# Attention on one Trainium2 core: the negated row maxima reach the queries by two DMAs instead of transposes on TensorE

## The chip, the cores and the metric

The kernel runs on one NeuronCore of a Trainium2 chip. Its engines are named as in the profile: PE (TensorE, the matrix products; PEld is its weight load), DVE (VectorE), ACT (ScalarE), POOL (GpSimd) and SP (SyncE, which here only issues DMAs). The metric is the device time of one execution, in microseconds (us), as the median of several runs.

## The reference

The input is `x` of shape (8, 192, 64, 64): 8 images, 192 channels, 4096 pixels. Two layers follow each other, each added to its input.

```
def _L0_conv_ref(x, w1, b1, a1, w2, b2, a2, wa, ba, aa):      # 1x1 convolutions to 24, 24 and 192 channels
    q = prelu(conv1x1(x, w1, b1), a1)
    k = prelu(conv1x1(x, w2, b2), a2)
    v = prelu(conv1x1(x, wa, ba), aa)
    q = q.reshape(b, -1, hw).transpose(0, 2, 1)
    k = k.reshape(b, -1, hw)
    score = jax.nn.softmax(jnp.einsum('bnc,bcm->bnm', q, k), axis=2)
    v = v.reshape(b, c, hw).transpose(0, 2, 1)
    out = jnp.einsum('bnm,bmc->bnc', score, v)
...
x = x + _L0_conv_ref(_gn(x), ...)     # _gn: normalization over groups of 6 channels
x = x + _L1_conv_ref(_gn(x), ...)     # pointwise: four small linear maps with tanh between them, then
                                      # abs(sigmoid(sign * upper) - sigmoid(sign * lower)), at least 1e-6
```

So layer 0 is attention over 4096 pixels per image, with 24 channels of queries and keys and 192 of values, all in float32. Layer 1 is elementwise work with per-channel weights (below: the density).

## The kernel before

**Blocks and steps.** Each image has 8 blocks of 512 queries, so there are 64 blocks. A block takes 16 steps; a step handles 256 keys for the block's 512 queries. `scores` (L794) computes two products of 128 keys by 512 queries into PSUM, ACT takes their exponential (L798), and `attend` (L809) multiplies the exponentials with the values: 8 products of 128 queries by 193 columns, the last column being the sum of the row. The main loop runs the 1024 steps one after the other; the head before it prepares image 0, and the tail after it finishes the density of image 7.

**The maxima.** The softmax subtracts each query's maximum before the exponential. The maxima of a block are found ahead: in every step, `max_step` (L722, L730) computes 128 queries by 1024 keys, for the step that lies `LEAD` = 22 steps further, and DVE reduces them. After 16 such steps a block's maxima are complete, 6 steps before its first scores. The queries lie in a tile `q` with 128 partitions: four groups of 32, each with 24 channels and one row more, row 24 of the group (`CR`). The keys have a 1 in that row, so a score product over 25 rows adds whatever stands there. The negated maximum of each query has to get there.

**How it gets there now.** `max_end` (L744) plans three things. `collect`: DVE reduces 16 columns to 4 and negates (L750), and copies the result into columns 24, 56, 88, 120 of a tile `negmax` that is zero otherwise (L753). `turn`: PE transposes `negmax` in four 128x128 pieces into a PSUM bank (L759). `add`: DVE adds this bank to the block's columns of `q` (L765), where only the four rows 24 get anything but zero. `turn` needs a free half of a PSUM turn tile, so it goes through `job`, a queue of pieces of work (keys L634, values L683, transposed outputs L842) of which `start_job` starts one a step.

**What sets the order.** The order on every engine is written by the program itself. `at(t, fn, cost, act, pe)` puts a function into step `t`; `work_off` runs the step's functions, starts one job, issues the loads for which a buffer is free, and lets the density take what is left: `density_step` gives DVE and ACT as much density work as a credit allows, which falls with the planned cost of the other work and rises with the time planned for PE. Nothing else reorders. SP issues its DMAs strictly in this order: loads of `x` for statistics, keys and values (`xi`, L109) and for the residual (`xc`, L109, four DMAs of 384 KB at once), stores of finished keys and queries (L649, L650), loads of the queries of two blocks (`queries`, L665), and stores of the output (L1374). A tile's reader waits for the DMA that wrote it.

**Other places that the change touches.** `weights` folds the normalization into the convolutions, once per image: `mb` (L554) is the mean of each channel copied along 128 columns, and `products` multiplies it with the weights of the values (L566). The partitions hold the 64 rows of channels twice; `products` uses the first 64. Before the first products, the head waits for the statistics of image 0.

Of the kernel before, what the change touches and what calls it, by code (L numbers as in the profile page):

```python
# [9 lines left out]
F32 = mybir.dt.float32  # L10
AF = mybir.ActivationFunctionType
ALU = mybir.AluOpType
# [5 lines left out]
def kernel(  # L18
# [43 lines left out]
    nc = tc.nc  # L62

    B, C, H, W = x.shape
    N = H * W
    CR = w1t.shape[1]
    F = 512
# [4 lines left out]
    R = C // 3  # L72
# [9 lines left out]
    const = ctx.enter_context(tc.tile_pool(name="const", bufs=1))  # L82
# [7 lines left out]
    dram = ctx.enter_context(  # L90
        tc.tile_pool(name="dram", bufs=1, space=bass.MemoryType.DRAM)
    )
    dens = ctx.enter_context(tc.tile_pool(name="dens", bufs=1))
    ps_sc = ctx.enter_context(tc.tile_pool(name="ps_sc", bufs=1, space=PSUM))
    ps_mx = ctx.enter_context(tc.tile_pool(name="ps_mx", bufs=1, space=PSUM))
# [3 lines left out]
    for i in range(2):  # L99
        turn = ps_b.tile([128, 2, F], F32, tag=f"b{i}", name=f"b{i}")  # L100
# [17 lines left out]
    for i in range(3):  # L118
        t = xin.tile([128, 3, P], F32, tag=f"xi{i}", name=f"xi{i}")
# [20 lines left out]
    ident = const.tile([128, 128], F32, name="ident")  # L140
    make_identity(nc, ident)


    gavg = const.tile([128, 128], F32, name="gavg")
    gq = gavg.rearrange("p (s a b) -> p s a b", s=2, b=2)
    idq = ident.rearrange("p (s a b) -> p s a b", s=2, b=2)
# [31 lines left out]
    for i in range(2):  # L178
        nc.vector.tensor_reduce(
            out=bb[i], in_=ident[:, 64 * i + CR : 64 * i + 64 : 32], axis=AX.X, op=ALU.add  # L180
# [6 lines left out]
    for s in range(2):  # L187
        p = slice(R * s, R * s + R)
# [4 lines left out]
    for i in range(2):  # L193
# [3 lines left out]
        for k in range(2):  # L197
            a = a2 if k == i else a1
            nc.scalar.dma_start(
                out=slope[i][64 * k : 64 * k + 64], in_=a.partition_broadcast(64)  # L200
# [3 lines left out]
    def spread():  # L204

        for i in range(2):
            for k in range(4):
                at = slice(32 * k, 32 * k + CR)
                p = slice(R * (k % 2), R * (k % 2) + R)
                nc.gpsimd.tensor_copy(wr[i][p, :, at], (s2 if k // 2 == i else s1)[p])  # L210
        for g in range(3):
            nc.gpsimd.tensor_copy(
                wa_sb[:, g, :].rearrange("p (h r) -> p h r", h=3),
                sa[:, g, :].rearrange("p (r h) -> p h r", h=3),
            )
        for s in range(2):
            p = slice(R * s, R * s + 1)
            nc.gpsimd.tensor_copy(
                ba_row[p].rearrange("p (h r) -> p h r", h=3),
                sb[p].rearrange("p (r h) -> p h r", h=3),  # L220
            )

    def negatives():
        for i, a in enumerate((*slope, vslope)):
            nc.vector.tensor_scalar(nslope[:, i : i + 1], a, -1.0, None, ALU.mult)

    negmax = const.tile([128, 4, 128], F32, name="negmax")
    nc.gpsimd.memset(negmax, 0.0)


    mm = const.tile([128, 3, 24], F32, name="mm")
# [2 lines left out]
    for src, dst, at, n in (  # L234
# [4 lines left out]
        for s in range(2):  # L239
            nc.sync.dma_start(  # L240
                out=dst[R * s : R * s + R, :, at : at + n],
                in_=src.rearrange("(r g) i j -> r g (i j)", g=3),
# [84 lines left out]
    now = [0]  # L327

    def at(t, fn, cost=0.0, act=0.0, pe=0.0):

        due.setdefault(max(t, now[0]), []).append((fn, cost, act, pe))
# [13 lines left out]
    def job(make, hold, rank=3, banks=1, cols=0):  # L345

        jobs.append((rank, make, hold, banks, cols))
        jobs.sort(key=lambda j: j[0])  # L350
# [9 lines left out]
    for k in "ab":  # L360
        pair = []
        for i in range(2):
            u = work.tile([128, 2 * C], F32, tag=f"pr{k}{i}", name=f"pr{k}{i}")
# [7 lines left out]
    def spotted():  # L371

        n, i = spot[0]

        def write(inst):
            tc.declare_no_dep(inst.ins, group=f"turn{n}{1 - i}", reason="reads the other bank")

        def read(inst):
            tc.add_to_no_dep_group(f"turn{n}{i}", inst.ins)

        return write, read
# [159 lines left out]
    wf = {}  # L541

    def weights(b, then):
        res = norms[b, 0]
        cell = {}

        def scale():
            for k, src in ((0, wr[0]), (1, wr[1]), ("v", wa_sb)):
                d = wf[k, b] = fold.tile(
                    [128, 3, src.shape[2]], F32, tag=f"w{k}", name=f"w{k}_{b}"  # L550
                )
                nc.scalar.activation(d, src, AF.Copy, scale=res[:, 1:2])
            mb = cell["mb"] = fold.tile([128, 128], F32, tag="mb", name=f"mb_{b}")
            nc.vector.tensor_copy(mb, res[:, 0:1].to_broadcast([128, 128]))  # L554

        def products():
            pf = cell["pf"]
            p = slice(0, R)
            for i in range(2):
                for g in range(3):  # L560
                    cell["write"](nc.tensor.matmul(
                        pf[:, 2 * i : 2 * i + 2], lhsT=wf[i, b][:, g, :], rhs=res[:, 0:2],
                        start=g == 0, stop=g == 2,
                    ))
            for g in range(3):
                cell["write"](nc.tensor.matmul(  # L566
                    pf[:, 4 : 4 + C], lhsT=cell["mb"][p], rhs=wf["v", b][p, g, :],
                    start=g == 0, stop=g == 2,
                ))

        def offsets():
            pf = cell["pf"]
            for i in range(2):
                d = wf["b", i, b] = fold.tile([128, 2], F32, tag=f"b{i}", name=f"b{i}_{b}")
                cell["read"](nc.vector.tensor_tensor(
                    d[:, 0:1], bb[i], pf[:, 2 * i : 2 * i + 1], ALU.subtract
                ))
                nc.vector.tensor_scalar(d[:, 1:2], d[:, 0:1], -1.0, None, ALU.mult)
            d = wf["ba", b] = fold.tile([128, C], F32, tag="ba", name=f"ba_{b}")
            cell["read"](nc.vector.tensor_tensor(d, ba_row, pf[:, 4 : 4 + C], ALU.subtract))  # L580
            then()

        at(now[0] + 1, scale, 0.3, 2.0)

        def make(pf, _):
            cell["pf"] = pf
            cell["write"], cell["read"] = spotted()
            return [(0, products, 0.0, 0.0, 2.0), (1, offsets, 1.0, 0.0, 0.0)]

        at(now[0] + 3, lambda: job(make, 1))  # L590
# [5 lines left out]
    for i in range(NC + 2):  # L596
        v = vpool.tile([128, 2, 4, C + 1], F32, tag=f"v{i}", name=f"v{i}")
        nc.gpsimd.memset(v[:, :, :, C : C + 1], 1.0)
        vtiles.append(v)
    qt = {}  # L600
# [18 lines left out]
    for i in range(2):  # L619
        t = dram.tile([NC, 64, F], F32, tag=f"qd{i}", name=f"qd{i}")  # L620
# [113 lines left out]
    def max_step(m):  # L734
        b, n, j, k = place(m)
        if b >= B:
            return
        sc = ps_mx.tile([128, 2, F], F32, tag="mx", name=f"mx_{m}")
        max_products(b, n, j, k, sc)
        max_reduce(b, n, j, k, sc)  # L740
        if m % STEPS == STEPS - 1:
            max_end(b, n)

    def max_end(b, n):  # L744
        rm = small.tile([128, 4], F32, tag="rn", name=f"rn_{b}_{n}")
        nm = negmax
        cell = {}

        def collect():
            nc.vector.tensor_reduce(  # L750
                out=rm, in_=rowmax.pop((b, n)), axis=AX.X, op=ALU.max, negate=True
            )
            nc.vector.tensor_copy(nm[:, :, CR::32], rm.unsqueeze(2).to_broadcast([128, 4, 4]))  # L753

        def turn():
            pt = cell["pt"]
            for t in range(4):
                cell["write"](
                    nc.tensor.transpose(pt[:, t * 128 : (t + 1) * 128], nm[:, t, :], ident)  # L759
                )  # L760

        def add():
            u = (n % 2) * 256
            q = qt[b, n // 2][:, :, u : u + 256]
            cell["read"](nc.vector.tensor_tensor(  # L765
                q, q, cell["pt"].rearrange("p (s t) -> p s t", s=2), ALU.add
            ))
            made.add(("max", b, n))

        def make(pt, _):  # L770
            cell["pt"] = pt
            cell["write"], cell["read"] = spotted()
            return [(0, turn, 0.0, 0.0, 0.8), (1, add, 0.7, 0.0, 0.0)]

        at(now[0], collect, 0.4)
        at(now[0] + 1, lambda: job(make, 1, 0))


    ex = {}
# [711 lines left out]
    while todo or ahead:  # L1491
        if todo:
            make, d, *k = todo.pop(0)
            make(0, d, *k, "first", lambda: None)
        pair = list(zip(others, ahead.popleft() if ahead else ()))
        if pair and len(homes) > 2:
            del homes[2:]
        for t, (n, j, k) in pair:
            max_products(0, n, j, k, t)
        for t, (n, j, k) in pair:  # L1500
            max_reduce(0, n, j, k, t)
        if (0, 3, 3) in [i for _, i in pair]:
            max_end(0, 0)
        if ("qd", 0, 1) in made and (0, 0) not in qt:
            queries(0, 0)
        go_on()
# [9 lines left out]
    for t in range(last):  # L1516
        b = t // IMG
# [21 lines left out]
    t = last  # L1539
# [42 lines left out]
```

## Time and profile before

| what | value |
|---|---|
| runs | 4770.4, 4772.68 and 4775.0 us; median 4772.68 us |
| the profiled execution | 4769.2 us, of which the span of instructions is 4767.4 us |
| first score product starts | 89.9 us |
| main loop to the start of the last score product | 4419.2 us |
| PE busy | 4627.5 us, 97% of the span |
| DVE busy | 4166.2 us, 87% |
| ACT busy | 3220.1 us, 68% |
| transposes of the maxima (L759) | 256 products, 38.4 us of busy time |
| their addition to the queries (L765) | 64 instructions, 43.4 us of DVE |
| DMA queue of SP | 133.81 MB, 11.5% of the 16 engines' time |

A row of the profile's groups reads: line, engine, operation, output and inputs by name, shapes and how often; then the busy time, the mean duration of one in nanoseconds, and the engine's idle time in front of it with what ended it. A float32 product appears as two MATMUL rows (and two LDWEIGHTS), a transpose as one. The timeline gives start, duration and count; equal instructions that follow each other are merged into one row.

### The profile page before, as it was taken

How to read it: one execution, taken by the hardware profiler on the slowest of the kernel's cores; microseconds unless marked ns; L12 is line 12 of the kernel's file. 1: busy time of each engine (PE TensorE's matmuls, PEld its weight loads, DVE VectorE, ACT ScalarE, POOL GpSimd, SP SyncE). 2: the span in 40 equal slices, each digit the busy share in tenths (PEclk: the TensorE clock that was granted, in tenths of full speed). 3: DMA queues.
4: the chain of work that ended last, by engine and by line, in shares of the span. 5: the costliest groups of instructions: out<-in, count | busy, mean ns of one | idle time of the engine just before them, and what ended most of it. 6: DMA issues, size and time to landing. Idle time of an engine off the chain costs nothing.

```text
span 4767.4 us, 68896 instructions
## 1 busy us (share of the span) xinstructions
PE 4627.5 (97%) x28344; PEld 3428.8 (72%) x28344; DVE 4166.2 (87%) x4289; ACT 3220.1 (68%) x3687; POOL 865.6 (18%) x842
## 2 busy tenths in 40 slices
PE   7999999999999999999999999999999999999685
PEld 5777777777777777777777777777777777777332
DVE  5433359999999999999999999999999999998898
ACT  2332246767677777776777767777777777778786
POOL 0000001212222212221212222132222122232100
PEclk9999999999999999999999999999999999999797
DMA  2101020111100111110110111001111101000000
GB/s 59 41 18 30 18 48 14 33 30 30 44 25 25 37 39 34 27 40 12 36 46 26 30 41 36 28 16 40 36 38 33 31 16 27 10 5 23 9 14 13
DMA packets 109328, 138.58 MB, mean 29 GB/s; under 512 B 17107, under 2 KB 82133, under 8 KB 109013
## 3 DMA queue, kind: packets, MB, share of 16 engines
q1 hardware_dynamic: 107776, 133.81, 11.5%
q8 instruction: 222, 3.64, 0.3%
q14 instruction: 94, 0.76, 0.1%
q10 hardware_dynamic: 1236, 0.37, 0.0%
HBM read 100.58 MB, written 29.36 MB: 27 GB/s over the span
## 4 chain that ended last, share of the span: by engine, by line
PE 93%; DVE 3%; ACT 2%; issue 1%; DMA 0%; POOL 0%; ACTq 0%; POOLq 0%; SPq 0%; DVEq 0%
PE b L809 60%; PE sc L794 22%; PE b L683 4%; DVE d L1094 2%; PE b L634 2%; PE mx L722 1%; PE b L1033 1%; PE b L842 1%; PE mx_tail L1033 1%; PE b L759 1%; ACT d L1087 0%; PE sc_tail L1033 0%; ACT d L1062 0%; ACT e L798 0%; ACT d L1077 0%
## 5 line engine op out<-in xcount | busy, mean ns | idle before, releaser
L809 PEld LDWEIGHTS b<-v,e 128*128 128x128 f32 x16384 | 2650.6, 190 | 776.4 <-issue 765.1
L809 PE MATMUL b<-v,e 128*128 128x193 f32 x16384 | 2954.5, 334 | 0.0
L798 ACT ACTIVATE e<-sc 128x1024 f32<-128x1024 f32 x1024 | 1045.4, 1021 | 1320.2 <-PE mx L722 1282.7
L730 DVE TENSOR_REDUCE rm<-mx 128x1 f32<-128x1024 f32 x1002 | 1223.4, 1221 | 476.6 <-PE mx L722 470.3
L794 PE MATMUL sc<-q,k 25*128 25x512 f32 x4096 | 1154.6, 640 | 4.1 <-ACT e L798 3.8
L722 PE MATMUL mx<-k,q 24*128 24x512 f32 x4008 | 1129.8, 640 | 0.0
L1094 DVE SCALAR_TENSOR_TENSOR d<-d,lc,d 128x1024 f32<-128x1024 f32 x756 | 977.3, 1302 | 16.8 <-ACT d L1071 4.8
L1094 DVE SCALAR_TENSOR_TENSOR d<-d,wsp,d 128x1024 f32<-128x1024 f32 x684 | 877.4, 1286 | 44.9 <-ACT d L1087 36.5
L1277 POOL MEMSET pause<- 128x1 f32 x408 | 39.9, 98 | 3585.2 <-DVE d L1094 3585.2
L1094 DVE SCALAR_TENSOR_TENSOR d<-d,tf,d 128x1024 f32<-128x1024 f32 x540 | 685.4, 1288 | 2.3 <-ACT d L1077 2.3
L1077 ACT ACTIVATE d<-d 128x1024 f32<-128x1024 f32 x540 | 566.8, 1052 | 40.1 <-DVE d L1094 39.6
L794 PEld LDWEIGHTS sc<-q,k 25*128 25x128 f32 x4096 | 306.2, 182 | 229.6 <-issue 188.9
L1087 ACT ACTIVATE d<-d,cb,wsp 128x1024 f32<-128x1024 f32 x348 | 429.3, 1235 | 1.6 <-DVE d L1094 0.6
L1062 ACT ACTIVATE d<-xc,bn,wn 128x1024 f32<-128x1024 f32 x288 | 354.3, 1234 | 0.8 <-issue 0.8
L1125 POOL TENSOR_TENSOR d<-d,d 128x512 f32<-128x512 f32 x168 | 335.9, 2000 | 37.1 <-ACT d L1119 35.7
L1071 ACT ACTIVATE d<-xc,bn,wn 128x1024 f32<-128x1024 f32 x252 | 311.4, 1236 | 0.0
L722 PEld LDWEIGHTS mx<-k,q 24*128 24x128 f32 x4008 | 299.6, 182 | 9.1 <-DVE rm L730 8.2
L1312 POOL TENSOR_TENSOR d<-d,d 128x512 f32<-128x512 f32 x80 | 170.1, 2127 | 0.0
L1324 POOL TENSOR_TENSOR d<-d,d 128x512 f32<-128x512 f32 x80 | 169.9, 2124 | 0.5 <-issue 0.5
L1332 POOL TENSOR_TENSOR d<-d,d 128x512 f32<-128x512 f32 x80 | 159.2, 1990 | 1.8
L683 PE MATMUL b<-wv,xi 64*128 64x192 f32 x1344 | 139.5, 340 | 0.0
L683 PEld LDWEIGHTS b<-wv,xi 64*128 64x128 f32 x1344 | 106.5, 186 | 25.4 <-issue 23.6
(158 smaller groups left out, 2288.6 us busy)
## 6 DMA issues: line engine op xcount, KB each, us to landing
xi<-in_x_dram SPq DMA_DIRECT2D x280, 192.0 KB, 3.7
xc<-in_x_dram SPq DMA_DIRECT2D x64, 384.0 KB, 7.5
out_dram<-xc SPq DMA_DIRECT2D x94, 256.0 KB, 3.2
q<-qd SPq DMA_DIRECT2D x128, 128.0 KB, 2.7
k<-kq SPq DMA_DIRECT2D x64, 64.0 KB, 1.9
qd<-kq SPq DMA_DIRECT2D x64, 64.0 KB, 2.1
d<-in_x_dram SPq DMA_DIRECT2D x16, 192.0 KB, 4.2
out_dram<-xc SPq DMA_DIRECT2D x4, 128.0 KB
```

The lines of the kernel that those rows point to most:

```text
L683: nc.tensor.matmul(pv[:, s, 0:C], lhsT=t[p, g, k * 128 : k * 128 + 128] if g < 3 else one_row[p], rhs=wf["v", b][p, g, :] if g < 3 else wf ...
L722: nc.tensor.matmul(sc[:, s, :], lhsT=tile_of(qt[b, n // 2], n, j)[r], rhs=kt[b][r, u : u + F], start=True, stop=True,)
L730: nc.vector.tensor_reduce(out=rowmax[b, n][:, j, k : k + 1], in_=sc, axis=AX.XY, op=ALU.max)
L794: nc.tensor.matmul(sc[:, s, :], lhsT=kt[b][r, k : k + 128], rhs=qt[b, n // 2][r, :, u : u + 256], start=True, stop=True,)
L798: return lambda: nc.scalar.activation(e, sc, AF.Exp)
L809: nc.tensor.matmul(a[:, j, 0 : C + 1], lhsT=e[:, s, j * 128 : j * 128 + 128], rhs=v[:, s, p % 4, :], start=p == 0 and s == 0 and j % 2 == ...
L1062: nc.scalar.activation(self.buf[k], self.src(), AF.Tanh, bias=bn[:, s, g, 0, i : i + 1], scale=wn[:, g, 0, i : i + 1],)
L1071: nc.scalar.activation(self.buf[k], self.src(), AF.Identity, bias=bn[:, s, g, 1, i : i + 1], scale=wn[:, g, 1, i : i + 1],)
L1077: nc.scalar.activation(self.buf[k], self.buf["l", k[1], k[2]], AF.Tanh)
L1087: nc.scalar.activation(self.buf[k], self.buf["l", n - 1, 0], AF.Identity, bias=offset, scale=wsp[:, g, w : w + 1],)
L1094: nc.vector.scalar_tensor_tensor(dst, src, factor, dst, ALU.mult, ALU.add)
L1125: return nc.gpsimd.tensor_tensor(z[:, n], z[:, n], dst[:, n], ALU.add)
```

## The change

`max_end` no longer uses PE. `collect` keeps only the reduction. Two steps later SP stores the 128x4 result to a DRAM tile of 4x128 (`nd`, two in turn), and four steps after `collect` SP loads it into row 24 of each of the four groups of `q`, one DMA for each. The transposes, the addition, the copy and `negmax` are gone, and with them one job a block. In the head, 14 products of the identity with itself, 384 columns each, are put in front of everything on PE; nothing reads them. `mb` is now half of the mean, and `products` sums over all 128 partitions instead of 64, which gives the same.

```diff
+    idle = ps_mx.tile([128, 2, F], F32, tag="mx", name="idle")
+    for i in range(14):
+        nc.tensor.matmul(
+            idle[:, i % 2, 0:384], lhsT=ident, rhs=ident.unsqueeze(1).to_broadcast([128, 3, 128]),
+            start=True, stop=True,
+        )
...
-    negmax = const.tile([128, 4, 128], F32, name="negmax")
-    nc.gpsimd.memset(negmax, 0.0)
...
-            nc.vector.tensor_copy(mb, res[:, 0:1].to_broadcast([128, 128]))
+            nc.vector.tensor_scalar(
+                mb, res[:, 0:1].to_broadcast([128, 128]), 0.5, None, ALU.mult
+            )
...
-                    pf[:, 4 : 4 + C], lhsT=cell["mb"][p], rhs=wf["v", b][p, g, :],
+                    pf[:, 4 : 4 + C], lhsT=cell["mb"], rhs=wf["v", b][:, g, :],
...
+    nd = []
+    for i in range(2):
+        t = dram.tile([4, 128], F32, tag=f"nd{i}", name=f"nd{i}")
+        nd.append(t)
+
     def max_end(b, n):
...
-            nc.vector.tensor_copy(nm[:, :, CR::32], rm.unsqueeze(2).to_broadcast([128, 4, 4]))
-
-        def turn():
-            pt = cell["pt"]
-            for t in range(4):
-                cell["write"](
-                    nc.tensor.transpose(pt[:, t * 128 : (t + 1) * 128], nm[:, t, :], ident)
-                )
-
-        def add():
-            u = (n % 2) * 256
-            q = qt[b, n // 2][:, :, u : u + 256]
-            cell["read"](nc.vector.tensor_tensor(
-                q, q, cell["pt"].rearrange("p (s t) -> p s t", s=2), ALU.add
-            ))
+        d = nd[n % 2]
+
+        def store():
+            nc.sync.dma_start(out=d.rearrange("j p -> p j"), in_=rm)
+
+        def spread():
+            u = (n % 2) * 256
+            for k in range(4):
+                nc.sync.dma_start(
+                    out=qt[b, n // 2][32 * k + CR : 32 * k + CR + 1, :, u : u + 256],
+                    in_=d.rearrange("(o s) p -> o s p", o=1).rearrange(
+                        "o (s a) p -> o s (a p)", s=2
+                    ),
+                )
             made.add(("max", b, n))
 
-        def make(pt, _):
-            cell["pt"] = pt
-            cell["write"], cell["read"] = spotted()
-            return [(0, turn, 0.0, 0.0, 0.8), (1, add, 0.7, 0.0, 0.0)]
-
-        at(now[0], collect, 0.4)
-        at(now[0] + 1, lambda: job(make, 1, 0))
+        at(now[0], collect, 0.3)
+        at(now[0] + 2, store)
+        at(now[0] + 4, spread)
```

More of the change, by code (lines that the diff above doesn't have):

```diff
@@ L553, in scale @@
             mb = cell["mb"] = fold.tile([128, 128], F32, tag="mb", name=f"mb_{b}")
-            nc.vector.tensor_copy(mb, res[:, 0:1].to_broadcast([128, 128]))
+            nc.vector.tensor_scalar(
+                mb, res[:, 0:1].to_broadcast([128, 128]), 0.5, None, ALU.mult
+            )
         def products():
             pf = cell["pf"]
-            p = slice(0, R)
             for i in range(2):
@@ L742, in max_step @@
             max_end(b, n)
+    nd = []
+    for i in range(2):
+        t = dram.tile([4, 128], F32, tag=f"nd{i}", name=f"nd{i}")
+        nd.append(t)
     def max_end(b, n):
         rm = small.tile([128, 4], F32, tag="rn", name=f"rn_{b}_{n}")
-        nm = negmax
-        cell = {}
         def collect():
```

## The prediction

> **What bounds the kernel now.** First the busy times and the chain that ended last (page, parts 1 and 4):
>
> ```profile
> PE 4627.5 (97%) x28344; PEld 3428.8 (72%) x28344; DVE 4166.2 (87%) x4289; ACT 3220.1 (68%) x3687; POOL 865.6 (18%) x842
> PE 93%; DVE 3%; ACT 2%; issue 1%; DMA 0%; POOL 0%; ACTq 0%; POOLq 0%; SPq 0%; DVEq 0%
> ```
>
> The chain runs on PE for 93%, and no DMA is on it. Busy shares alone don't tell what a removed product is worth, so the timeline of PE is read around one `turn`:
>
> ```profile
> 410.19 0.70 PE L794 MATMUL sc<-q,k 25*128 25x512 f32 x2
> ...
> 413.98 0.60 PE L759 MATMUL b<-ident,negmax 128*128 128x128 f32 x4
> 414.51 0.70 PE L794 MATMUL sc<-q,k 25*128 25x512 f32 x2
> ...
> 415.58 2.88 PE L809 MATMUL b<-v,e 128*128 128x193 f32 x16
> 418.39 0.70 PE L794 MATMUL sc<-q,k 25*128 25x512 f32 x2
> ```
>
> A step from scores to scores takes 418.39 - 414.51 = 3.88 us, the one with the transposes 414.51 - 410.19 = 4.32. In this stretch PE waits for nobody, so a `turn` costs its 0.44 us in full.
>
> Then what goes or comes, from the groups:
>
> ```profile
> L765 DVE TENSOR_TENSOR q<-q,b 128x512 f32<-128x512 f32 x64 | 43.4, 679 | 0.0
> L753 DVE COPY negmax<-rn 128x16 f32<-128x16 f32 x64 | 16.2, 253 | 2.2
> L759 PE MATMUL b<-ident,negmax 128*128 128x128 f32 x256 | 38.4, 273 | 1.1 <-DVE negmax L753 1.1
> ```
>
> The 38.4 us are not the saving; the 64 steps are.
>
> Last the queue that the new DMAs enter, at block 6 of image 3: SP's timeline, then the landings there, in a window around 1584 (block 6 of image 2), and overall:
>
> ```profile
> 2121.66 1.12 SPq L1374 DMA_DIRECT2D out_dram<-xc  x2
> 2125.49 3.10 SPq L109 DMA_DIRECT2D xc<-in_x_dram  x4
> 2130.86 1.72 SPq L665 DMA_DIRECT2D q<-qd  x4
> ```
> ```profile
> xc<-in_x_dram SPq DMA_DIRECT2D x4, 384.0 KB, 7.9
> ```
> ```profile
> q<-qd SPq DMA_DIRECT2D x4, 128.0 KB, 6.6
> ```
> ```profile
> q<-qd SPq DMA_DIRECT2D x128, 128.0 KB, 2.7
> ```
>
> Seen over the span DMA is 11.5% busy, but here the engines are full for over 10 us: the same load of queries lands after 6.6 us behind the `xc` loads and after 2.7 us in the median. A DMA on SP's queue waits for the bytes in front of it.
>
> **The sum, part by part** (against the profiled execution, 4769.2 us, of which the span is 4767.4; the median of the runs is 4772.7, 3.5 higher).
>
> *Transposes.* 64 x 0.436 = -27.9 us, since the step is longer by that and PE is the bound (0.436 = 4.32 - 3.88 before rounding). The bounds are -38.4 (their busy time) and 0.
>
> *DVE.* 43.4 + 16.2 = 59.6 us of work go. Nearly all lay beside PE's products: DVE is 87% busy, PE 97%. It counts where DVE ends last. Near the start of block 1 of image 3, between 1781.8 and 1794.6, the three steps last 4.1, 4.2 and 4.5 us with DVE busy for 3.93, 4.20 and 4.50 of them: some 1.2 us over 3 x 3.88. Images 2 to 6 look alike there, so 5 x 1.2 = 6 us bounds the gain, 0 is the other end; the add stands just ahead of these steps, so I take half, -3.
>
> *Five DMAs a block.* One store of 128x4 elements of 4 bytes, four loads of two runs of 1 KB. Issuing costs SP about 0.6 (as the head's small loads: 8 in 5.15 us) + 4 x 0.43 = 2.3 us, on an engine that mostly waits. `collect` ends about 22 us before the block's first scores, e.g. `rn` at 2112.7 and scores at 2134.23. The store is put in two steps later, the load four, so that the load may go when SP has passed all that was planned up to two steps before the scores, and the store has landed. The store has no like in the trace. A 64 KB store of queries lands after 2.1 us; the head's loads of 64 single elements after 3.1. With 3 to 4 us for the store and 2.3 for a load, most blocks keep 6 to 20 us. Even at 8 x (3.1 - 2.1) = 8 us for 512 single elements on top only two or three us appear in a dozen blocks; so this is kept for the range, up to +20.
>
> What is exposed are the blocks where SP's queue has the refill of `xc` between store and load: two output stores, which wait for DVE (2121.66), and four loads that wait for these stores (2125.49). In the changed order this holds for blocks 2 and 6 of images 2 to 6. At block 6 of image 3 the new loads are issued from 2128.6 to 2130.3, behind 1.57 MB. The fourth `xc` load, issued about 2128.0, lands 7.9 us later, at 2135.9; the bytes alone (at the 205 to 230 GB/s that the window shows, from 2126.2) are through by 2133.4, and an engine of the 16 that finishes early lets a small load through at about 2134.5. The scores stood at 2134.23 and come 0.44 earlier for the `turn` that was between: 2133.8. So they wait 0.7 to 2.3, I take 1.5. Block 6 of images 2, 4, 5, 6 has the same spacing (first `xc` load 8.7 to 8.8 us before the scores): 5 x 1.5 = 7.5. Block 2 of images 3 to 6 has 10.3 to 12.3 us there, so 0 to 0.8 each; image 7 has a store behind an `xc` refill, 0 to 1.2: together 1.5. Block 2 of image 2 loses more: its refill is planned one step later than before, 3.9 us, so its first `xc` load comes some 8 us before the scores, or 6.5 when the half-clock stretch below is gone: 4. Sum +13; bounds 0 (small loads slip through) and +30 (ten times 3).
>
> *Clock.* The granted clock fell to half twice in the loop, after stretches of small products (L561, then L566 on 64 of 128 rows):
>
> ```profile
> 1295.50:1298.90 3.40, 3.40 (x28) 2.71 (x27) 3.37 (x4) 0.00 (x0) 0.00 (x0) 1.00 0.48 110
> 1298.90:1302.30 3.40, 3.40 (x13) 2.86 (x10) 2.88 (x8) 2.71 (x3) 0.00 (x0) 0.50 0.27 91
> 90.60:94.00 3.40, 1.15 (x10) 0.31 (x8) 0.62 (x1) 2.56 (x3) 0.00 (x0) 1.00 0.00 0
> 94.00:97.40 3.40, 3.40 (x13) 2.85 (x10) 1.23 (x1) 1.02 (x1) 0.00 (x0) 0.50 0.00 0
> ```
>
> (busy us and count of each engine, then granted clock). The 16 MATMULs of `attend` take 4.28 us there instead of 2.88, a step 1.6 us more. L566 on all rows should spare one of the two for good (-1.6; the other lies under the wait of image 2). But a PE that waits 2.25 us lost its clock too (90.6 to 97.4). Waits of 1.5 us do it seldom, one of 4 nearly surely: +2.8. Net +1.2; bounds -3.3 and +16 (ten waits, each with its half-clock stretch).
>
> *Head.* The idle products start at 1.3 us, when `ident` is there, and take at most 14 x 1.47 = 20.5 us (6 instructions of 256 columns take 2.93 us at the start: 0.98 a product), so they end before PE's first work at 23.0 and delay nothing. If they kept the clock up, L561, L566 and the first two groups of L634 (2.72, 2.28, 2.93, 1.97 us) would take the 1.40, 1.24, 1.46, 1.46 seen later: -4.3. But at full clock they end near 12 us, and 11 us of idle follow, where 2.25 were enough to lose the clock: no gain from them, -1 for L566 on all rows, which may raise the clock one stretch earlier. The Trainium skill ("TensorE: Matmul & The Clock Gate", Part 1: The HAM clock gate) says the same with its window of about 3.4 us, after which an idle PE is halved again; the half-clock stretches here last 3.4 us, so the trace agrees, and by it the head gains nothing from the idle products.
>
> Sum: -27.9 - 3 + 13 + 1.2 - 1 = -17.7: 4751.5 on the scale of the profiled execution, 4755 for the median of runs.
>
> **Rivals.** *Nothing is late.* Without waits and their clock losses: -27.9 - 3 - 1.6 - 1 = -33.5, 4739. For it: two runs of 1 KB need one or two engines, and nine of the ten blocks are within 2.5 us of being in time. Against it: the 6.6 us of the query loads. The Trainium skill ("DMA: Bandwidth & Descriptors", Queues, rings and completion order) has each engine take descriptors in the order of the ring, which the 6.6 against 2.7 us bears out; by that rule this rival falls.
>
> *The waits eat the gain.* The ten blocks wait 2.5 to 3 each: 28 us, and the time stays within 10 us of before: 4765 to 4780. For it: 2135.9 as the landing plus a small DMA's own time.
>
> *Slower.* Each of those waits also costs a half-clock stretch: ten waits of 3 us and ten times 1.6 make 46; -27.9 - 3 - 1 + 46 = +14, 4787. It decides from waits of about 2.2 us, the length that lost the clock at 91 us. Or the store of single elements is slow: the Trainium skill (same page, Rules for kernel authors) warns that a non-contiguous last dimension becomes one descriptor per element; the trace shows no such store. From 12 us for it on, a dozen more blocks would wait.
>
> *The change doesn't do what it says:* the idle products do nothing for the time, by the argument above; this is inside the forecast.
>
> **How the numbers follow.** Forecast (some loads late by 1 to 2 us): 0.60; nothing late: 0.13; waits eat the gain: 0.14; slower: 0.13. About 0.2% (9.5 us) is what a measurement of this kernel can tell from no change. The forecast's own range is 4744 to 4767, of which 0.50 lies beyond 9.5 us and 0.10 within. Faster: 0.50 + 0.13 = 0.63; same: 0.10 + 0.12 = 0.22; slower: 0.13 + 0.02 = 0.15. The range reaches from the second case to the third: 4738 to 4778.
>
> **What would show it.** In the profile after: steps of 3.88 us where 4.32 stood; no L759 or L765 rows; the first scores of block 6 in images 2 to 6 idle on the loads from `nd` for about 1.5 us, block 2 of image 2 for about 4, nobody else; the clock at half after the longest of these; PE's products before 32 us as slow as before. Wrong if most blocks wait for `nd` (the store is dear), or if none does.

## The result and the profile after

| | median | runs | ratio to before, with its 95% interval |
|---|---|---|---|
| before | 4772.01 us | 9, from 4769.06 to 4775.08 | |
| changed | 4761.65 us | 9, from 4757.60 to 4763.59 | 0.9976, 0.9967 to 0.9986 |

The change gains 10.4 us, or 0.24%. The forecast was 4755, so 6.7 us of the expected gain are missing. (A block takes five DMAs, one store and four loads; the two of the title are these two kinds.) The rest of this document splits the time of a profile into three parts: up to the first score product ("head"), from there to the start of the last one ("loop"), and what follows ("tail"):

| us | head | loop | tail | span |
|---|---|---|---|---|
| before | 89.9 | 4329.2 | 348.3 | 4767.4 |
| changed | 87.1 | 4321.1 | 349.0 | 4757.2 |

(The 4419.2 us in the table ahead of the prediction is the time at which the last score product starts, 4419.1 by the timeline, and not the length of the loop.)

First, busy times and the chain that ended last in the changed kernel (its page, parts 1 and 4):

```profile
PE 4609.7 (97%) x28116; PEld 3403.4 (72%) x28116; DVE 4125.5 (87%) x4161; ACT 3218.6 (68%) x3687; POOL 869.8 (18%) x841
PE 89%; DVE 5%; ACT 3%; DMA 2%; issue 1%; SPq 0%; POOL 0%; ACTq 0%; POOLq 0%; DVEq 0%
```

PE still bounds the kernel, but its share of the chain is 89% where it was 93%, and 2% are now DMA. The timeline of PE around the place where the `turn` of the shown block was:

```profile
405.94 0.70 PE L802 MATMUL sc<-q,k 25*128 25x512 f32 x2
...
409.82 0.70 PE L802 MATMUL sc<-q,k 25*128 25x512 f32 x2
...
413.71 0.70 PE L802 MATMUL sc<-q,k 25*128 25x512 f32 x2
```

Both steps last 3.88 us; the step of 4.32 is gone. What came instead is among the waits, of PE and then of SP's queue (waiting engine, line, what for; us in total, times, longest):

```profile
PE sc L802 <- DMA q<-nd: 17.6, 7, 5.7
```
```profile
SPq L774 <- DMA nd<-rn: 380.8, 47, 11.4
```

Scores wait seven times for the loads of the maxima, 17.6 us in all: 5.6 at block 2 of image 2, 5.7 at block 2 of image 7, and about 1.3 each at block 6 of images 2 to 6. SP itself waits 380.8 us, in 47 blocks some 8 us each, for the store to land before it may issue the loads. In all 64 blocks at least 7.9 us lie between store and loads. SP's timeline shows both, first an undisturbed block, then block 2 of image 2 and block 2 of image 7:

```profile
404.75 0.38 SPq L769 DMA_DIRECT2D nd<-rn  x1
413.00 2.40 SPq L774 DMA_DIRECT2D q<-nd  x4
```
```profile
1275.80 0.38 SPq L769 DMA_DIRECT2D nd<-rn  x1
1291.10 1.18 SPq L1382 DMA_DIRECT2D out_dram<-xc  x2
1294.92 2.56 SPq L109 DMA_DIRECT2D xc<-in_x_dram  x4
1297.57 2.38 SPq L774 DMA_DIRECT2D q<-nd  x4
```
```profile
4014.68 2.56 SPq L109 DMA_DIRECT2D xc<-in_x_dram  x4
4017.27 0.60 SPq L769 DMA_DIRECT2D nd<-rn  x1
4029.37 2.39 SPq L774 DMA_DIRECT2D q<-nd  x4
```

From store to loads it takes 8.2 us where nothing is in the way. At 1297.57 the store is long done, and the loads follow the four refills of 384 KB. At 4017.27 the store itself stands behind the refill, and the loads are let go 12.1 us later. The clock then adds to the two long waits. First the score that waits at block 2 of image 2, then the windows around it (busy us and count of PE, PEld, DVE, ACT and POOL, granted clock, DMA share, GB/s):

```profile
1304.83 1.41 PE L802 MATMUL sc<-q,k 25*128 25x512 f32 x2 [5.63 <-DMA q<-nd]
```
```profile
1296.40:1299.80 3.40, 2.80 (x16) 2.50 (x16) 3.40 (x4) 1.97 (x2) 0.00 (x0) 1.00 0.98 228
1299.80:1303.20 3.40, 0.00 (x0) 0.00 (x0) 0.40 (x1) 0.00 (x0) 0.00 (x0) 1.00 1.04 217
1303.20:1306.60 3.40, 1.77 (x8) 0.73 (x8) 0.00 (x0) 0.00 (x0) 0.00 (x0) 0.50 0.99 205
1306.60:1310.00 3.40, 3.40 (x13) 2.97 (x10) 2.81 (x3) 2.81 (x3) 0.00 (x0) 0.50 0.64 186
```

PE stands still in the second window, and the clock is at half in the two that follow, 6.8 us. While the DMA engines move 205 to 228 GB/s, mostly for the refill, the four loads of 2 KB, all issued by 1299.95, do not let the score go before 1304.83. In the loop the clock is at half for 20.4 us; before it was 10.2. The two products at 1304.83 take 1.41 us at half clock, where the same two took 0.70 above; so half of such time is taken as lost: 10.2 us against 5.1. (This is an estimate. In the first half-clock window behind a long wait PE still waits for 1.6 to 2.3 us, so that about 1 us a wait is counted twice.)

The loop's -8.1 us are then accounted for: 63 turns of 0.436 that lie in it -27.5; waits +17.6; clock +5.1; the products of the means -0.6 (their step fell from 6.28 to 6.20 us in seven images); the rest, -2.7, is what remains for DVE and for what these estimates miss.

### The profile page after: what moved, and what is told of

Same layout as the page of the kernel before. It is cut to its first block, busy times and chain, and to the rows that moved or that the text cites. A ratio compares the mean times of both kernels' runs of the same rounds, so it can differ in the third digit from the quotient of the medians.

```text
span 4757.2 us, 68763 instructions
## 1 busy us (share of the span) xinstructions
PE 4609.7 (97%) x28116; PEld 3403.4 (72%) x28116; DVE 4125.5 (87%) x4161; ACT 3218.6 (68%) x3687; POOL 869.8 (18%) x841
## 2 busy tenths in 40 slices
DMA packets 144145, 139.25 MB, mean 29 GB/s; under 512 B 51410, under 2 KB 116948, under 8 KB 143828
## 3 DMA queue, kind: packets, MB, share of 16 engines
q1 hardware_dynamic: 142592, 134.47, 12.1%
## 4 chain that ended last, share of the span: by engine, by line
PE 89%; DVE 5%; ACT 3%; DMA 2%; issue 1%; SPq 0%; POOL 0%; ACTq 0%; POOLq 0%; DVEq 0%
PE b L817 57%; PE sc L802 21%; PE b L690 4%; DVE d L1102 3%; PE b L641 2%; PE b L1041 1%; PE mx L729 1%; DMA q<-nd 1%; PE mx_tail L1041 1%; PE b L850 1%; DVE rm L737 1%; DMA out_dram<-xc 0%; ACT d L1095 0%; PE sc_tail L1041 0%; SPq L109 0%
## 5 line engine op out<-in xcount | busy, mean ns | idle before, releaser
L802 PE MATMUL sc<-q,k 25*128 25x512 f32 x4096 | 1157.7, 641 | 23.6 <-DMA q<-nd 17.6
```

What stands on the lines that cost most here:

```text
L802: nc.tensor.matmul(sc[:, s, :], lhsT=kt[b][r, k : k + 128], rhs=qt[b, n // 2][r, :, u : u + 256], start=True, stop=True,)
```

## The experiments

The theory to be tested: the turns are worth the 28 us, and what is missing went into scores that wait for loads behind a refill, and into the clock after them. The rival: five more DMAs a block cost by themselves, wherever they stand, above all the slow store. The runs in full, with the loop of each profile, the scores' waits for the maxima in it, and its time at half clock. Each ratio is against runs of the kernel before taken along with it; they ran on three chips, on which the kernel before has medians of 4770.98 (e1 to e4), 4772.39 (e5 to e8) and 4772.08 us (e9 to e11).

| run | median us | ratio, 95% interval | loop | waits | half clock |
|---|---|---|---|---|---|
| before | 4772.0 | | 4329.2 | 0 | 10.2 |
| changed | 4761.65 | 0.9976 (0.9967 to 0.9986) | 4321.1 | 17.6 | 20.4 |
| e1_early | 4751.80 | 0.9959 (0.9945 to 0.9973) | 4311.1 | 0 | 23.8 |
| e2_refill_later | 4733.27 | 0.9921 (0.9908 to 0.9935) | 4293.1 | 0 | 0 |
| e3_no_dma | 4734.63 | 0.9924 (0.9911 to 0.9938) | 4295.5 | 0 | 3.4 |
| e4_other_parts | 4766.44 | 0.9989 (0.9981 to 0.9998) | 4325.1 | 0 | 3.4 |
| e5_no_idle | 4778.61 | 1.0012 (1.0003 to 1.0022) | 4338.0 | 27.5 | 34.0 |
| e6_runs_of_16 | 4754.95 | 0.9962 (0.9948 to 0.9977) | 4316.0 | 12.2 | 17.0 |
| e7_early_runs | 4735.34 | 0.9920 (0.9905 to 0.9935) | 4295.8 | 0 | 3.4 |
| e8_before_refill_later | 4769.08 | 0.9991 (0.9982 to 1.0001) | 4327.9 | 0 | 13.6 |
| e9_later_no_idle | 4735.07 | 0.9921 (0.9904 to 0.9937) | 4296.1 | 0 | 6.8 |
| e10_idle_1 | 4767.79 | 0.9992 (0.9983 to 1.0001) | 4328.9 | 21.5 | 27.2 |
| e11_idle_20 | 4762.70 | 0.9980 (0.9970 to 0.9989) | 4323.7 | 19.2 | 20.4 |

**Held refill.** The loads of `xc` are not issued in steps 10 to 13 of a block, so that the loads of the maxima go ahead of them (`stream[0]` is true in the main loop).

```diff
         for kind, fn in list(loads):
-            if free[kind] > 0 and kind not in held:
+            wait = kind == "xc" and stream[0] and 10 <= t % STEPS <= 13
+            if free[kind] > 0 and kind not in held and not wait:
```

> The changed kernel, with the refill of xc held back where it would be issued in steps 10 to 13 of a block, until step 14, behind the load from nd; the output stores stay. Theory A: the waits of blocks 2 and 6 go, 4740 us (4735 to 4747). Rival B: the store is as slow as before, so image 2 and 7 block 2 still wait about 5 us; 4750 us. Rival C: 4758 to 4765 us. A later xc may delay the residual of a block by three steps, which by both theories costs nothing on PE.

It took 4733.27 us, the shortest of all runs here, well under both kernels and a little under theory A's range. No score waits for the maxima and the clock is never at half in the loop. SP's timeline of this run at block 6 of image 3:

```profile
2104.04 1.12 SPq L1383 DMA_DIRECT2D out_dram<-xc  x2
2105.27 2.75 SPq L775 DMA_DIRECT2D q<-nd  x4
2108.14 2.55 SPq L109 DMA_DIRECT2D xc<-in_x_dram  x4
```

The loads stand ahead of the refill. The loop is 28.0 us shorter than in the changed kernel; its waits and half of its half-clock time were 17.6 + 10.2 = 27.8. That is the theory's number, but for 1.7 us: half of the stretch at half clock that the changed kernel has at the start of its loop (91.4 us), behind a wait of 2.60 us for ACT and not for a load. This run has that wait too and, alone of the thirteen, keeps its clock there, which is luck.

**No DMAs at all.** The maxima are still reduced, but neither stored nor loaded, so nothing is subtracted before the exponential.

```diff
-        def store():
...
         def spread():
-            u = (n % 2) * 256
-            for k in range(4):
-                nc.sync.dma_start(
...
             made.add(("max", b, n))
...
-        at(now[0] + 2, store)
         at(now[0] + 4, spread)
```

> The changed kernel without the store and the four loads: row 24 of the queries stays zero, no maximum is subtracted, the order of all else is the same. It is the bound for anything done to the DMAs. Theory A: 17.6 us of waits and about 5 us of clock are saved, 4739 us (4734 to 4744), within 3 us of the kernel with the early store. If the maxima's DMAs cost more than their visible waits (contention with other loads, SP held up), it is faster than the early store by over 5 us.

4734.63 us: the held refill, with all five DMAs a block, is as fast (its interval covers this one's ratio). The DMAs cost nothing that these runs can tell where nobody waits for them. Here the refill is not held back, and the loop is 25.6 us shorter than in the changed kernel; the waits and the half clock behind them were 17.6 + 8.5 = 26.1. So the theory's number does not rest on the held refill alone.

**The control for the held refill.** The same two lines in the kernel before.

> The kernel before with the refill of the image's rows held back from steps 10 to 13 of a block, the edit by which the changed kernel came to 4733 us. Theory A (holding it back is worth nothing where no load of the maxima stands behind it): 4768 to 4774 us. Rival B (the held refill is a gain of its own, by the transfers it keeps apart or the clock): 4745 to 4762 us, in which case that much of the 28 us is not the waits of the scores.

4769.08 us, and the interval includes 1. So no more than the 0.2% that its interval leaves is a gain of holding the refill as such. A small one is not excluded: what is left of its loop without half the half clock is 4321.1 us, where the kernel before has 4324.1.

**Early order.** Store and loads are both put ahead of the refill, with one step between them.

```diff
-        at(now[0] + 2, store)
-        at(now[0] + 4, spread)
+        at(now[0], store)
+        at(now[0] + 1, spread)
```

> The changed kernel (4761.65 us, before 4772.0), with the store in the step of collect and the load one step later, so that both stand in SP's order ahead of the output stores and the xc refill. Theory A (the gain went to the scores that wait for the loads from nd behind the refill, 17.6 us in 7 waits, and to the clock lost after the long ones, some 5 us): the waits are gone, the time is 4739 us (4734 to 4745). Rival B (the 512 single elements of the store are the cost wherever it stands: in the changed kernel an undisturbed store at 404.8 us is followed by its load only 8.2 us later): SP now stands still for about 8 us in every block with loads and stores of others behind it, some of these come late, and the time is 4750 to 4765 us. Rival C (the waits cost nothing in the end, since DVE or ACT bound the steps behind them): 4758 to 4765 us.

4751.80 us: the waits for the maxima are gone as expected, but 17 us of the gain did not come: the range that rival B gave. Steps at the end of block 0 in images 1 to 6 last 5.6 to 8.0 us. Image 3, by the timelines of SP, of DVE and of PE:

```profile
1764.83 0.39 SPq L769 DMA_DIRECT2D nd<-rn  x1
1765.27 1.20 SPq L109 DMA_DIRECT2D xi<-in_x_dram  x2
1774.76 2.40 SPq L774 DMA_DIRECT2D q<-nd  x4
1777.27 1.24 SPq L109 DMA_DIRECT2D xi<-in_x_dram  x2
```
```profile
1778.08 0.56 DVE L461 BATCH_NORM_STATS2 st<-xi 128x6 f32<-128x384 f32 x1 [2.00 <-DMA xi<-in_x_dram]
```
```profile
1782.49 1.13 PE L729 MATMUL mx<-k,q 24*128 24x512 f32 x4 [1.24 <-DVE rm L737]
1783.55 4.56 PE L817 MATMUL b<-v,e 128*128 128x193 f32 x16
```

SP stands at the loads (1774.76) until the store has landed. The next image's rows (1777.27) are queued behind them; DVE waits 2.00 us for them, its reduction of the maxima comes late, PE waits 1.24 us, and the clock falls: `attend` takes 4.56 us in place of 2.88. So the store does hold up the queue. In the changed kernel the last rows go out at 1767.54 at this place, ahead of the store at 1768.77, and nothing but the loads of the maxima stands behind it; DVE waits for no rows there.

**A store in longer runs.** The scratch tile becomes 128 x 4, so the store writes 128 runs of 16 bytes in place of 512 single elements. The loads move the same bytes, but in another order of the queries, so other numbers than a query's own maximum are subtracted.

```diff
-        t = dram.tile([4, 128], F32, tag=f"nd{i}", name=f"nd{i}")
+        t = dram.tile([128, 4], F32, tag=f"nd{i}", name=f"nd{i}")
...
-            nc.sync.dma_start(out=d.rearrange("j p -> p j"), in_=rm)
+            nc.sync.dma_start(out=d, in_=rm)
...
-                    in_=d.rearrange("(o s) p -> o s p", o=1).rearrange(
-                        "o (s a) p -> o s (a p)", s=2
-                    ),
+                    in_=d.rearrange("(o s p) j -> o s (p j)", o=1, s=2),
```

> The changed kernel with its scratch tile turned to 128 x 4, so that the store writes 128 runs of 16 bytes in place of 512 single elements; the loads, still five DMAs a block of the same bytes, then hand the queries' maxima on in another order, so other numbers are subtracted than the queries' own maxima. Theory A (it is the store of single elements that takes the 8 us from store to loads): from the store to the loads 2 to 3 us in place of 8.2; SyncE's waits of the loads for the store fall from 380 us to under 130; the wait of block 2 in image 7 (5.7 us, behind a store that itself stood behind the refill) goes, that of block 2 in image 2 (5.6 us, behind the refill alone) stays; time 4752 to 4757 us. Rival B (the 8 us are the way to DRAM and back, whatever the runs): the gap stays above 7 us, both waits stay, 4759 to 4764 us.

4754.95 us. By SP's timeline of the same block as above, and its waits:

```profile
406.23 0.34 SPq L769 DMA_DIRECT2D nd<-rn  x1
408.00 2.41 SPq L774 DMA_DIRECT2D q<-nd  x4
```
```profile
SPq L774 <- DMA nd<-rn: 70.8, 38, 7.0
```

From store to loads it takes 1.8 us instead of 8.2, so some 6.5 us of the store are its single elements. At block 2 of image 7 the store still stands behind the refill, but the loads follow it after 7.7 us in place of 12.1 (4021.10 to 4028.80); the wait there has shrunk to 0.2 us, and those behind a refill alone stay: 12.2 us in place of 17.6. The packets of the whole program tell the same (DMA totals of the kernel before, the changed one, and this one):

```profile
DMA packets 109328, 138.58 MB, mean 29 GB/s; under 512 B 17107, under 2 KB 82133, under 8 KB 109013
```
```profile
DMA packets 144145, 139.25 MB, mean 29 GB/s; under 512 B 51410, under 2 KB 116948, under 8 KB 143828
```
```profile
DMA packets 119570, 139.25 MB, mean 29 GB/s; under 512 B 26835, under 2 KB 92373, under 8 KB 119253
```

144145 - 119570 = 24575, which is 64 times 512 - 128 = 384 packets, less one: a packet for each element in the one, for each run in the other. The Trainium skill ("DMA: Bandwidth & Descriptors", Rules for kernel authors) says that a last dimension that is not contiguous becomes a descriptor per element; these packet counts agree.

**Early order with such a store.** Both edits together.

> Stored in the step of the maxima and loaded one step later, as in the early run, but with the store in 128 runs of 16 bytes (other numbers subtracted, as in the run with the turned scratch tile). Theory A (the early run lost its 17 us because SyncE stood 8 us behind the store of single elements and the rows of the next image went out behind it, so that VectorE waited for them and TensorE for VectorE): SyncE is free 2 to 3 us after the store, no long step at the end of block 0 of images 1 to 6, 4733 to 4739 us. Rival B (it is the place of the loads, or their issue time, that holds the rows up, whatever the store takes): the long steps of 5.6 to 8 us at the end of block 0 stay, 4747 to 4753 us.

4735.34 us against 4751.80. SP's timeline at the same place of image 3:

```profile
1754.99 0.35 SPq L769 DMA_DIRECT2D nd<-rn  x1
1755.39 1.23 SPq L109 DMA_DIRECT2D xi<-in_x_dram  x2
1756.72 2.41 SPq L774 DMA_DIRECT2D q<-nd  x4
1759.23 1.24 SPq L109 DMA_DIRECT2D xi<-in_x_dram  x2
```

The rows now follow 4 us after the store, not 12, and the steps at the end of block 0 are as in the changed kernel (4.9 us at most). This is the whole of what the early order had lost: it was the time of the store, not the place of the loads.

**The other parts alone.** The kernel before, with the fourteen idle products and the halved means over 128 partitions.

> The kernel before, with the idle products in the head and the products over all 128 partitions (half of the mean), and the maxima still by transposes. Theory A: the head is faster by 1 to 2.5 us, and the two half-clock stretches behind L566 go (3.3 us): 4767 to 4770 us against 4772. If the clock phase alone set these stretches, no change: 4771 to 4773 us.

4766.44 us, a gain of 0.1%. The head is 0.9 us longer, where 1 to 2.5 less were expected. The loop is 4.1 us shorter: 7 x 0.08 = 0.6 by the products' step, and (10.2 - 3.4) / 2 = 3.4 by the clock. Both half-clock stretches after the products of the means (1298.9 and 2940.7 before) are gone, and so they are in every other run here that sums over 128 partitions, but for stretches behind a wait. The kernel before with the refill held has two such stretches, at other images (763.7 and 3487.6).

**Without the idle products.** The changed kernel less the fourteen.

> The changed kernel without the fourteen idle products of the head; all else as it is. Theory A (the idle products are worth nothing but a shift of the head of some us, since the kernel before with these products and the halved means alone had its first score at 90.8 us, 0.9 us later than before without them): 4758 to 4765 us, first score at 87 to 90 us, half clock gone between 16 and 33 us of the head. Rival B (the idle products gave the 2.8 us by which the first score came earlier): first score at 89.9 us and 4764.5 us. Rival C (the clock they wake up carries on into the loop): 4768 us and more half clock after 90 us.

4778.61 us, 17 us slower than the changed kernel, and a little slower than before. None of the three theories had this; C is nearest, with more half clock in the loop, but the clock alone is not it. Its loop has 9.9 us more of waits and 13.6 more at half clock, which make 16.7 of the 16.9 us by which it is longer. SP's timeline and PE's at block 6 of image 3 in this run show from where:

```profile
2113.86 0.38 SPq L761 DMA_DIRECT2D nd<-rn  x1
2122.55 4.71 SPq L1374 DMA_DIRECT2D out_dram<-xc  x2
2129.90 2.56 SPq L109 DMA_DIRECT2D xc<-in_x_dram  x4
2132.56 2.40 SPq L766 DMA_DIRECT2D q<-nd  x4
```
```profile
2140.13 1.46 PE L794 MATMUL sc<-q,k 25*128 25x512 f32 x2 [4.95 <-DMA q<-nd]
```

The two output stores take SP 4.71 us to issue, where the changed kernel needs 1.12 at this place. The refill waits for them and the loads for the refill, so this score waits 4.95 us in place of 1.57. Why the issue is slow the profile does not say. It goes with the build: all ten executions lie between 4775.94 and 4782.64 us, and the run with the longer runs of the store, on the same chip, has no such issue. Three more runs ask whether it is the products' warmth or this.

**One and twenty idle products**, by the loop's count in the changed kernel (`range(14)`).

> The changed kernel with one idle product in place of fourteen: about 1 us of work at the start, too little to matter for the clock of what follows 20 us later. Theory A (the 17 us are a matter of when issues on SyncE and refills fall, not of warmth): the time may lie anywhere between 4755 and 4780 us, and follows from the trace: scores' waits for the maxima plus half of the half-clock time inside the loop account for the difference to the changed kernel within 3 us. Rival B (the warmth is what counts): 4774 to 4783 us, as without any.

> The changed kernel with twenty idle products in place of fourteen, about 5 us more of them, ending near 18 us, ahead of the first product of the norms at 23 us. Theory A (when issues fall, not warmth): anywhere between 4755 and 4780 us, again accounted for by the scores' waits and the half clock in the loop. Rival B (more warmth, more gain or the same): 4757 to 4763 us.

4767.79 and 4762.70 us (of the ten executions with twenty, one took 13747 us, at a mean granted clock of 0.343 where the others have 0.985; nothing here tells why, and the ratio leaves it out). With one, 10.8 of the 17 us are back, though the clock of its head is no better: its profile records no rise to full clock before 35.9 us, as that without any records none before 35.3. With twenty both theories fit. Its waits and half the half clock are 21.5 + 13.6 = 35.1 us against 27.8 in the changed kernel: +7.3, and the loop is 7.8 longer. With twenty they are +1.6, and the loop is 2.6 longer. In the run with one, too, the pairs of output stores before the refill are slow to issue at block 6 of images 2 and 3 (3.97 us at 1571.3, 2.83 at 2120.0), the same two places as without any; with fourteen or twenty no single issue of an output store in the loop took over 1.7. Nor is it the lack of idle products alone: the kernel before has none, and no such issue over 1.41.

**Held refill without the idle products.** The two edits together.

> The changed kernel with the refill held back and without the fourteen idle products: no score waits for the maxima any more, so a late DMA has nothing to lengthen. Theory A (the 17 us that the changed kernel lost without the idle products were lost in scores that wait behind a refill, which two slow issues of an output store on SyncE pushed 3.5 us further back, and in the half clock behind them): 4731 to 4738 us, within 4 us of the kernel with refill held back and idle products (4733.3). Rival B (the idle products are worth 17 us by themselves): 4746 to 4753 us.

4735.07 us, the same as with them (4733.27; the intervals cover each other). The slow issue is there again, but now harmless. SP's timeline of this run at block 6 of image 3:

```profile
2106.38 3.89 SPq L1375 DMA_DIRECT2D out_dram<-xc  x2
2110.37 2.71 SPq L767 DMA_DIRECT2D q<-nd  x4
2113.19 2.55 SPq L109 DMA_DIRECT2D xc<-in_x_dram  x4
```

So the idle products have no worth of their own that these runs can tell (1.8 us lie between the two). In the changed kernel they decide by 17 us, because there a late issue on SP lengthens waits that PE feels.

The table closes on this. Loop less waits less half the half clock is 4293.3 us in the changed kernel, and 4292.7 to 4295.3 in the eight runs of it from e2 to e11 in which SP holds up no rows (e2, e3, e5, e6, e7, e9, e10, e11). Only the early order with the slow store stands apart, at 4299.2: there PE waits for DVE as well.

## Why the prediction was right, and where its sizes were off

The forecast (faster by some 18 us, with a few loads late) named the right mechanism and places; 4761.65 lies in its range. It erred by 6.7 us. The largest misses were the late loads and their clock, 8.5 us together; that the total is nearer is in part luck, by a head that came out 2.8 us shorter where 1 was forecast, for reasons that the forecast did not have.

| term | predicted | measured in the profile |
|---|---|---|
| transposes | -27.9 | -27.5 in the loop (63 of 64); steps of 3.88 |
| DVE | -3 | -2.7, as the remainder |
| late loads | +13 | +17.6 |
| clock | +1.2 | +5.1 |
| products' step | not counted | -0.6 |
| head | -1 | -2.8 |
| tail | 0 | +0.7 |
| sum | -17.7 | -10.2 |

- **Transposes and DVE.** Reading the step and not the busy time of 38.4 us was the right choice: the runs without waits confirm it. Loop less waits less half the half clock falls from 4324.1 before to about 4294. For DVE -2.7 is a remainder, no larger than the 2.6 us by which the eight runs above differ in it. The three steps that the forecast named are shorter by 0.35 us in images 3 to 6 (12.46 us in place of 12.81) and by 0.7 in image 2, 2.1 us in all. Against the kernel before with the refill held, though, nothing remains: 4321.1 - 4293.1 = 28.0, and the turns and the products' step make 28.1. So the term has the right sign at the place named, and its size is not shown.
- **Late loads.** The blocks behind a refill were right: 6.3 us at the five blocks 6 (predicted 7.5), 5.6 at block 2 of image 2 (predicted 4). The miss is block 2 of image 7, taken at 0 to 1.2 and measured at 5.7. There the store stands behind the refill, and it was priced at 3 to 4 us; it takes 8.2 from store to loads undisturbed and 12.1 behind the refill. The text had kept "8 us for 512 single elements on top" for the range only; this was the value to take. With the store in longer runs that wait shrinks to 0.2. The dozen blocks feared with it did not wait: even with the 8 us the loads go out 11 us ahead of a block's first score in the median. Block 2 of images 3 to 6, with 0 to 0.8 each in the forecast, did not wait either.
- **Clock.** Sizes off both ways. The products of the means on all rows spare both of the old stretches, 3.4 us, where one and 1.6 were predicted. The waits cost 8.5 (17.0 us at half: 6.8, 3.4 and 6.8) where 2.8 were. Each of the two waits near 5.6 us brought two windows of 3.4 us at half, not one. How seldom a short wait loses the clock was judged rightly: in the five runs in which scores wait for the maxima the clock falls behind all 13 waits of 2.97 us or more, and behind 5 of the 25 of 0.28 to 1.82 us.
- **Head.** The first products were as slow as before, as said: L568 takes 2.72 us and L573 2.27, where L561 and L566 took 2.72 and 2.28. The granted clock, high at first with the idle products, is at half from 16.3 to 33.4 us, as the argument from the 11 us of idle wanted. Of the 2.8 us by which the first score came earlier, 1.6 are the 64th turn, which lies in the head: at 72.65 us its transposes wait 1.08 us for `negmax` (the wait in the row of L759 in the prediction) and the next product starts 0.56 later. The forecast had it at 0.44, like those in the loop, where PE waits for nobody. This wait is in the three profiles with transposes and in none of the ten without; from PE's first product that is not idle work to the first score it takes 66.8 to 67.3 us in the three and 64.0 to 66.1 in the ten. About as much as the remaining 1.2 us is gained by the next two groups, at L641 (2.12 and 1.46 us in place of 2.93 and 1.97), since the clock is full again at 33.4 and not at 36.0 us. This moment lies between 33.2 and 37.0 over the thirteen profiles, so whether the idle products or the products on all rows, for which the forecast took 1, have a part in it is not shown; without them the first score starts at 88.7 us.
- **Rivals.** "Nothing is late" fell for the changed kernel, but the time it was given, 4739, is near what the held refill reaches (4733). That rival was 6 us too high: with the refill held the loop has no half clock at all, which is worth 5.1 us where 1.6 were counted (1.7 of it by luck, as said), and the products' step 0.6 that was not, 4.1 of the 6. "The waits eat the gain" is what the kernel without idle products does: 27.5 us of waits and 17 lost to the clock, 4778.61. Slower with a half clock at every wait did not come: the 1.3 us waits at the blocks 6 brought one stretch in five blocks.
- **Idle products.** That they do nothing for the time holds within 2 us where nothing waits, and is wrong as a statement on the changed kernel, where leaving them out costs 17 us by another way than the clock of the head.

Open: why SP takes 2.3 to 4.2 us over one issue of an output store in some builds, and why the number of idle products changes this; no run tells the cause.

## What to carry to other kernels

A small DMA that replaced work of the bounding engine was free here only where nothing large stood before it on its queue and nothing urgent behind it: look for the refill between the store and its reader, and move that. Two lines that hold it back took this change from 0.24% to 0.79%. Count a store's packets before giving it a time, and look who is queued behind an engine that waits for it to land. Where a part that does no work moves the time, look first for waits that small shifts can lengthen, and repeat the comparison with those waits taken out.

## What the runs showed of the hardware that was not expected

A DMA of 512 single elements of 4 bytes to DRAM holds its readers for 8.2 us after its issue, the same 2 KB in 128 runs for 1.8. A PE that stood still for 5.6 us lost its full clock for two windows of 3.4 us, though the products were back during the first of them. At the start of the loop waits of 2.25 to 2.60 us lost it in twelve of thirteen profiles. Issuing the same pair of output stores took SP 1.12, 2.83, 3.89 or 4.71 us, at block 6 of image 3, in builds that differ only in the idle products of the head and the place of the refill.
